# A decoder layer on one core: priority offsets by kind of result, rank-16 factors loaded early, other buffers for the last squares

## The chip, the cores and the metric

The kernel runs on one NeuronCore of a Trainium2 chip. The core has five engines that run side by side, each through its own instructions in order: TensorE (PE, matmuls; its weight loads, PEld, run beside them), VectorE (DVE), ScalarE (ACT), GpSimd (POOL) and SyncE (SP), which here only issues transfers. ScalarE can issue transfers too, on a queue of its own. The transfers of all queues run on 16 DMA engines. The metric is the device time of one execution in microseconds (us); lower is better.

## The reference

`x` and `ctx` are (8, 512, 256), float32. One layer of a decoder, with a layer norm behind each of three parts:

```python
x = _layernorm(x + _L0_attn_ref(x, W_q, W_k, W_v, W_g, W_o, log_decay))
x = _layernorm(x + _L0_xattn_ref(x, ctx, ctx, mask, Wq, bq, Wk, bk, Wv, bv, Wo, bo))
x = _layernorm(x + _L0_ffn_ref(x, fast_b, w_fc, w_proj, u, v, gate))
```

The first part is a gated linear attention within chunks of 32 positions, with a decay mask. The second is a softmax attention from x to ctx with 16 heads of 64. The third is the part that most of the change touches:

```python
scale = clip(mean(abs(w), axis=1), 1e-5)          # _bitlinear
tern = clip(round(w / scale), -1, 1)
y = x @ (tern * scale).T
h = _bitlinear(x, w_fc) + gate * (x @ v.T @ fast_b.T @ u.T)   # rank 16
r = maximum(h, 0)
out = _bitlinear(r * r, w_proj)
```

`u` is (1024, 16), `v` (16, 256), `fast_b` (16, 16), `gate` a scalar.

## The kernel before

Most float32 operands are split into two float16 halves, a high and a low one, and a product is three float16 matmuls (`PASSES`), accumulated in PSUM. So nearly every result of PE is followed by a cast (the high half, mostly ScalarE or GpSimd) and a subtraction (the low half, VectorE or GpSimd).

The work is cut by batch `b` (8), pair of heads `p` (8) and quarter of the queries `qt` (4): 256 units, which the code also calls steps. A unit has two score groups of 128 queries by 512 keys (`scores`: matmuls `s`, a VectorE reduction that adds the mask and finds the minimum `nm`, exponentials `e` on ScalarE), a split of the probabilities into halves `ph` (`split_p`), a DMA transpose of `ph` into `pT`, and the matmuls with the values, `av` (`attend`), which run about four units later. Around these units four "fillers" hand out other work in small pieces: the projections of keys, queries and values (`fr`), the first attention and the loads of the next batch (`bg`), the output projection and FFN of the batch before (`bf`), and a part of the last output projection (`bw`). `PULL` says how much of each is handed out per unit. In the first batch `bf` holds the set-up of weights instead: `setup_wo` and `setup_ffn`. `setup_ffn` makes the ternary weights (`fct`, `pjt`), a scale by an f32 matmul (`ps2`), and from the rank-16 factors `sv`, `gt`, `ur`, `fb` the two stationary operands `vst` and `ust`.

The code does not emit instructions in the order in which it is written. A `Recorder` collects every operation with a priority (`nc.prio`, counted in units: a lower value is earlier), then `schedule` plays the program through with a cost per operation (`cost`) and, whenever an engine is free, gives it the ready operation of lowest priority; an operation is ready when what it reads is there and its buffers are free. Where VectorE's next operation would have to wait for the memory port that it shares with GpSimd, another may go ahead of it whose priority is up to `REACH` later. The order found so is then emitted (that is why every row of the profile names line 451), and the hardware keeps it. So a constant in this planner has no cost of its own on the chip; it only changes the order. `LATE` holds offsets by kind of work (`c` scores, `a` attend, `t` the score reduction, `w` the set-up, `o` output projection, `f` FFN, `d` the transposes, and so on); the offsets `t`, `x` and `e` and everything added by the change hold only for operations with a priority of zero or more, and the set-up before the units has negative ones.

Buffers: a tile with a tag comes out of a ring of that tag with a fixed number of buffers, which SBUF rings hand out in program order. `tmp2` has four, `t4` five, `pT` and `ph` three each (a buffer of either holds 4,096 float16 values per partition), `E` three.

SP's queue carries all DMA transposes and nearly all loads, in the planner's order. ScalarE's queue carries six loads at the start. The end of the kernel is written out by hand behind the loop over the units: `bf.drain()`, the last `attend`s (`rest`), `wo_tail` (output projection, layer norm and transposes by PE) and `ffn_tail` for the two halves of the last batch's queries, interleaved by `go`; `TP` has the priorities of these parts. In `ffn_tail`, each of eight blocks `j` of the hidden dimension gives `r4` (relu, in an `E` buffer), its square, and the halves `rhl`, and three blocks later the matmuls `pyl` read them.

Of the kernel before, what the change touches and what calls it, by code (L numbers as in the profile page):

```python
# [11 lines left out]
F16 = mybir.dt.float16  # L12
F32 = mybir.dt.float32
# [8 lines left out]
HID, RANK = 1024, 16  # L22
# [4 lines left out]
LAG = 4  # L27
BURST = 2
MARGIN = 0.0
REACH = 9.52  # L30
SPARE = 1
DLATE = 1.6
PTS = 3
PHS = 3
NWP = 4
TP = (0.35, 0.96, 1.15, 3.0, 0.5, 5.1)
STICK = 2.09
HOLD = 0.18
HIGH = ("apaa", "paaa", "papp")
LATE = {"k": 0.0, "q": 0.0, "v": 0.53, "w": -0.33, "l": -0.41, "o": -0.91, "f": 0.31, "s": 0.0, "a": 0.91, "t": 0.0, "x": 0.31, "e": 0.0, "c": -1.28, "d": -0.95}  # L40
PULL = {"k": 5.13, "l": 2.62, "w": 3.61, "f": 4.71, "g": 5.48}

PASSES = ((0, 0), (0, 1), (1, 0))

# [109 lines left out]
class Recorder:  # L154
# [34 lines left out]
    def add(self, engine, method, args, kw):  # L189
        ins, outs = [], []  # L190
        for n, x in enumerate(args):
            if isinstance(x, View):
                (outs if n == 0 or (method == "tensor_tensor_reduce" and n == 7) else ins).append(x)
        for k, x in kw.items():
            if isinstance(x, View):
                (outs if k == "accum_out" else ins).append(x)
        o = Op()
        o.engine, o.method, o.args, o.kw, o.prio = engine, method, args, kw, self.prio
        if engine in ("DVE", "ACT") and method[:3] != "dma" and self.prio >= 0:
            src = ins[0].t if ins else None  # L200
            if method == "tensor_tensor_reduce":
                o.prio += LATE["t"]
            elif method == "activation" and args[2] == AF.Exp:
                o.prio += LATE["x"]
            elif src is not None and src.pool[:2] == "ps":
                o.prio += LATE["e"]
        o.preds, o.succs, o.bufs, o.parts = {}, [], [], None
        self.cost(o, ins, outs)
        if self.joint is not None and self.joint:
            j = self.joint[0]  # L210
            j.parts.append(o)
            self.access(j, ins, outs)
            return o
        o.seq = len(self.ops)
        self.ops.append(o)
        self.access(o, ins, outs)
        if self.joint is not None:
            o.parts = [o]
            self.joint.append(o)
        return o  # L220
# [30 lines left out]
    def cost(self, o, ins, outs):  # L251

        n = max([int(np.prod(x.shape[1:])) for x in outs + ins] or [0]) if o.engine != "PE" else outs[0].idx.size
        psum = any(x.t.pool[:2] == "ps" for x in ins + outs)
        ones = sum(x.idx.size == 1 and x.t.free > 0 for x in ins)
        o.half, o.port = None, o.engine == "POOL"
        o.dma = o.method[:3] == "dma"
        if o.dma:
            x = (outs or ins)[0]
            if o.method == "dma_start_transpose":  # L260
                blocks = n / 128
                o.occ, o.lat = 0.1 * blocks + 0.4, 0.115 * blocks + 0.55
            else:
                size = {F32: 4, F16: 2}.get(x.t.dt, 1)
                o.occ, o.lat = 0.45, n * size * x.shape[0] / (380e3 if self.prio < 0 else 210e3) + (1.2 if size == 1 else 0.1)
        elif o.engine == "PE":
            o.occ = n / 2400 + 0.0025
            o.lat = o.occ + 0.17
            if ins[0].p1 - ins[0].p0 == 64:
                o.half = ins[0].p0  # L270
        elif o.engine == "DVE":
            lat = 0.145 + n * 1.042e-3
            if o.method == "tensor_tensor_reduce":
                o.occ, o.lat = 0.615, 0.8
                return
            if not psum and o.method in ("tensor_copy", "tensor_scalar") and n >= 512:
                lat = 0.12 + n * 0.62e-3
            if psum and ones and o.method == "scalar_tensor_tensor":
                lat += 0.065
            if n <= 8:  # L280
                lat = 0.19 if o.method == "reciprocal" else 0.175 if o.method == "bn_aggr" else 0.145
            o.occ, o.lat = lat - 0.085, lat
            o.port = not psum and o.method in ("tensor_tensor", "scalar_tensor_tensor", "tensor_scalar", "tensor_copy")
        elif o.engine == "ACT":
            lat = 0.165 + n * 0.83e-3 + (0.0 if psum else 0.04) + 0.07 * ones
            o.occ, o.lat = (lat + 0.01, lat + 0.12) if "accum_out" in o.kw else (lat - 0.11, lat)
        elif o.engine == "POOL":
            if o.method == "tensor_tensor":
                lat = 0.3 + n * 1.67e-3 if n <= 512 else 0.2 + n * 1.9e-3
                if o.args[3] == ALU.pow:  # L290
                    lat = 0.42 + 0.16 * n
            else:
                lat = 0.13 + n * 0.9e-3 if n > 512 else 0.92 if n == 256 and o.kw == {} and o.method == "tensor_scalar" and o.args[-1] == ALU.is_lt else 0.62 if n > 256 else 0.56 if n > 8 else 0.22 + n * 5e-3
            o.occ, o.lat = lat - 0.03, lat
# [178 lines left out]
def decoder_kernel(ctx: ExitStack, tc: tile.TileContext, ins: dict, out: bass.AP):  # L473
    nc = Recorder(tc.nc, tc)
# [9 lines left out]
    def t4(name, shape, dt=F16):  # L484
        return wk.tile(shape, dt, tag="t4", name=name, bufs=5)

    def tmp2(name, shape, dt=F32):
        return wk.tile(shape, dt, tag="tmp2", name=name, bufs=4)
# [157 lines left out]
    def absmean(sc, th, src, n, width, nm):  # L646
# [4 lines left out]
        nc.vector.tensor_scalar(th[:, 0:n], sc, 0.5, None, ALU.mult)  # L651
        nc.vector.tensor_scalar(th[:, n:2 * n], sc, -0.5, None, ALU.mult)

    def setup_ffn():
        sfc = cst.tile([128, 8], F32, name="sfc")
        for i in range(2):
# [35 lines left out]
        pb = misc("ps2")  # L692
# [2 lines left out]
        yield 6  # L695

        nc.vector.memset(vst, 0.0)
        sv = tmp2("sv", [128, 2, RANK])
        nc.sync.dma_start(sv, ins["vT"].rearrange("(c p) r -> p c r", p=128))
        split(vst[:, :, 0:RANK], vst[:, :, 96:96 + RANK], sv, WS)  # L700
        for g in (32, 64):
            nc.vector.tensor_copy(vst[:, :, g:g + RANK], vst[:, :, 0:RANK])

        gt = cst.tile([128, 1], F32, name="gt")
        nc.sync.dma_start(gt, ins["gate"].broadcast_to([128, 1]))
        rs = cst.tile([128, 8], F32, name="rs")
        nc.vector.reciprocal(rs, sfc)
        nc.vector.tensor_scalar(rs, rs, gt, None, ALU.mult)
        ur = tmp2("ur", [128, 8, RANK])
        nc.sync.dma_start(ur, ins["u"].rearrange("(c p) r -> p c r", p=128))  # L710
        nc.vector.tensor_tensor(ur, ur, rs.unsqueeze(2).broadcast_to([128, 8, RANK]), ALU.mult)
        uh = tmp2("uh", [128, 2, 8, RANK], F16)
        split(uh[:, 0], uh[:, 1], ur, 1.0)
        fb = cst.tile([RANK, RANK], F32, name="fb")
        nc.sync.dma_start(fb, ins["fast_b"])
        fbs = cst.tile([RANK, 2, 128], F16, name="fbs")
        nc.vector.memset(fbs, 0.0)
        split(fbs[:, 0, 0:RANK], fbs[:, 1, 0:RANK], fb, 1.0)
# [311 lines left out]
    def ffn_tail(b, i, base, step_):  # L1030
        row = rows[b]
        rh, py = {}, {}
        ts = slice(256 * i, 256 * i + 256)
        PL = 3
        for s_ in range(8 + PL):
            nc.prio = base + step_ * s_
            if s_ == 0:
                zst = ffn_z(b, ts, f"{b}_{i}", ("zst", "sph")[i])
            if s_ < 8:
                j = s_  # L1040
                r4 = ffn_h(b, j, ts, zst, f"{b}_{i}", True)
                hl = t4(f"rhl{i}{j}", [128, 2, 256])
                if i == 0 or j % 2:
                    nc.scalar.activation(r4, r4, AF.Square)
                else:
                    nc.vector.tensor_tensor(r4, r4, r4, ALU.mult)
                if j % 2:
                    nc.scalar.copy(hl[:, 0], r4)
                else:
                    nc.vector.tensor_copy(hl[:, 0], r4)  # L1050
                (nc.vector if j % 3 == 2 or (i == 1 and j == 7) else nc.gpsimd).tensor_tensor(hl[:, 1], r4, hl[:, 0], ALU.subtract)
                rh[j] = hl
            if s_ >= PL:
                j = s_ - PL
                if j == 0:
                    for t in range(2):
                        py[t] = misc(f"pyl{i}{t}")[:, :D]
                hl = rh.pop(j)
                for t in range(2):
                    for a in range(2):  # L1060
                        nc.tensor.matmul(py[t], hl[:, a, t * 128:(t + 1) * 128], tpj[:, j, :],
                                         start=(j == 0 and a == 0), stop=(j == 7 and a == 1))
            yield
# [168 lines left out]
    for p in range(2):  # L1232
# [4 lines left out]
        if p == 0:  # L1237
            setup_qkv(2, 0, N1, 0)
            run_all(gen_v(0, 0))
    nc.prio = -1.0  # L1240
    for i in (1, 2, 0):
        setup_qkv(i, N1, HID, 0)
    nc.prio = 0.0
# [3 lines left out]
    def at(i, off):  # L1247
        now[0], nc.prio = i, i + off
# [84 lines left out]
            if pend:  # L1333
                attend(pend.pop(0))

    at(U, 1)
    bf.drain()
    at(U, TP[0])
    rest(len(pend) - 4)
# [63 lines left out]
```

## Time and profile before

| | us |
|---|---|
| median of 3 runs (1057.99 to 1062.4) | 1061.06 |
| the profiled execution: its own time | 1061.94 |
| its span, first to last instruction | 1060.1 |
| PE busy | 998.2 |
| VectorE busy | 986.9 |
| ScalarE busy | 879.4 |
| GpSimd busy | 544.8 |
| transposes pT, 131 of them: issue to landing, median | 7.5 |
| load of u: issued at 108.95, issue to landing | 3.9 |
| load of vT: issued at 108.3, issue to landing | 2.1 |

The loads of the gate and of `fast_b` are issued at 16.8 and 18.3 us. The profiled execution's granted TensorE clock is 0.988 of full speed on average.

How to read it: times in the trace start with the span. Busy time leaves out issuing, branching and waiting. A group of the profile is named engine, operation, output <- inputs, without buffer numbers. "Idle before" is the time that an engine stood still just ahead of an instruction, with what ended it; "issue" means that nothing which the profile shows was waited for. "PEld" waits are those of the weight loads, which run ahead of the matmuls. An average over the span hides that the stages differ: the set-up and first batch (to about 160 us), six batches of some 122 us each in steady running, and the end of the last batch (from about 1010 us).

### The profile page before, as it was taken

What the parts mean: (1) busy time and instruction counts of PE and PEld (TensorE: products, weight loads), DVE (VectorE), ACT (ScalarE), POOL (GpSimd) and SP (SyncE); (2) the same over time, 40 slices, a digit from 0 to 9 for tenths busy, and PEclk for the clock granted to TensorE, in tenths of its full rate; (3) what the DMA queues carried; (4) which work ended last, traced back from release to release, by engine and by line L of the source; (5) the groups of instructions that cost most, each with busy time, mean ns of one, the idle gap of its engine ahead of it and who ended that gap; (6) DMA issues with size and microseconds to landing.
All of it is one profiled execution on the core that took longest, in us unless ns stands there. A gap on an engine that the chain in (4) does not pass through costs nothing.

```text
span 1060.1 us, 29949 instructions
## 1 busy us (share of the span) xinstructions
PE 998.2 (94%) x11976; PEld 639.3 (60%) x11976; DVE 986.9 (93%) x2101; ACT 879.4 (83%) x1876; POOL 544.8 (51%) x513
## 2 busy tenths in 40 slices
PE   7986889999999999999999999999999999999986
PEld 4644545665666656665666656766567656665664
DVE  7999989999999989999899989999899998998976
ACT  7787778889977998789977898879977889878836
POOL 0251282256841596245861577426962548443635
PEclk9999989999999999999999999999999999999989
DMA  8289799999999999989999999999999999999861
GB/s 306 99 147 186 133 214 186 164 180 191 186 185 189 174 179 168 207 155 189 185 184 204 162 185 179 192 189 156 195 163 214 154 185 170 187 167 201 138 115 41
DMA packets 646636, 185.65 MB, mean 175 GB/s; under 512 B 628448, under 2 KB 641376, under 8 KB 646496
## 3 DMA queue, kind: packets, MB, share of 16 engines
q1 hardware_dynamic: 645632, 183.42, 95.6%
q8 instruction: 93, 1.52, 0.6%
q10 hardware_dynamic: 864, 0.32, 0.1%
q14 instruction: 47, 0.39, 0.1%
HBM read 21.18 MB, written 4.19 MB: 24 GB/s over the span
## 4 chain that ended last, share of the span: by engine, by line
PE 41%; ACT 17%; DVE 17%; DMA 12%; issue 6%; POOL 4%; SPq 2%; ACTq 0%; POOLq 0%; DVEq 0%
PE av L451 8%; PE s L451 8%; DMA pT<-ph 6%; ACT e L451 6%; DVE s L451 5%; DVE ph L451 5%; PE pk L451 4%; PE pq L451 4%; PE pwo L451 4%; ACT r L451 4%; PE py L451 3%; PE pvv L451 3%; ACT ph L451 3%; SPq L451 2%; DVE W L451 2%
## 5 line engine op out<-in xcount | busy, mean ns | idle before, releaser
L451 ACT ACTIVATE e<-s,nm 128x512 f32<-128x512 f32 x512 | 354.4, 705 | 100.7 <-DVE nm L451 83.3
L451 DVE SCALAR_TENSOR_TENSOR ph<-e,ph 128x1024 f16<-128x1024 f32 x256 | 330.6, 1298 | 27.6 <-ACT ph L451 25.2
L451 DVE CUSTOM_DVE_ANT_0 s<-s,mb 128x512 f32<-128x512 f32 x512 | 342.3, 710 | 6.1 <-PE s L451 4.5
L451 PEld LDWEIGHTS <-pT 128*128 128x128 f16 x6144 | 198.7, 99 | 59.5 <-issue 29.5
L451 PE MATMUL av<-v,pT 128*128 128x64 f16 x6144 | 213.2, 194 | 12.4 <-DMA pT<-ph 12.2
L451 PE MATMUL s<-W 64*128 64x512 f16 x1536 | 205.6, 379 | 12.5 <-ACT e L451 10.8
L451 ACT ACTIVATE ph<-e 128x1024 f16<-128x1024 f32 x186 | 200.0, 1081 | 2.4 <-DMA pT<-ph 0.3
L451 POOL TENSOR_SCALAR ph<-e 128x1024 f16<-128x1024 f32 x70 | 84.8, 1211 | 227.3 <-ACT e L451 214.7
L451 PEld LDWEIGHTS <-W 64*128 64x128 f16 x1536 | 64.2, 94 | 110.4 <-issue 59.4
L451 PEld LDWEIGHTS <-wqkv 128*128 128x128 f16 x768 | 70.3, 98 | 82.6 <-issue 18.0
L451 POOL TENSOR_TENSOR oh<-of,oh 128x512 f16<-128x512 f32 x62 | 86.6, 1396 | 65.0 <-ACT oh L451 63.1
L451 ACT ACTIVATION_READ_ACCUMULATOR e<-s,nm 128x1 f32 x512 | 113.5, 222 | 0.0
L451 PE MATMUL pk<-ctxh,wqkv 128*128 128x512 f16 x384 | 103.0, 382 | 6.2 <-POOL ctxh L451 6.1
L451 PE MATMUL pvv<-wqkv,ctxh 128*128 128x256 f16 x768 | 102.0, 274 | 0.3 <-DVE v L451 0.3
L451 POOL TENSOR_TENSOR rh<-r,rh 128x512 f16<-128x512 f32 x56 | 75.1, 1345 | 52.4 <-ACT rh L451 52.4
L451 PE MATMUL pq<-x1T,wqkv 128*128 128x512 f16 x384 | 97.2, 380 | 0.5 <-DVE bob L451 0.3
L451 PEld LDWEIGHTS <-ctxh 128*128 128x128 f16 x768 | 71.4, 98 | 26.1 <-issue 13.0
L451 PEld LDWEIGHTS <-oT 128*128 128x128 f16 x768 | 73.8, 100 | 20.8 <-issue 5.3
L451 PE MATMUL pwo<-wo,oT 128*128 128x256 f16 x672 | 84.2, 276 | 0.4 <-ACT e L451 0.4
L451 DVE DVE_READ_ACCUMULATOR2_ANT nm<- 128x1 f32 x512 | 72.4, 141 | 0.0
L451 PE MATMUL ph<-x2T,tfc 128*128 128x512 f16 (+1 forms) x288 | 68.4, 356 | 0.3 <-ACT r L451 0.3
L451 PE MATMUL py<-tpj,rh 128*128 128x256 f16 x448 | 58.4, 273 | 0.0
(190 smaller groups left out, 1492.4 us busy)
## 6 DMA issues: line engine op xcount, KB each, us to landing
row<-in_x SPq DMA_DIRECT2D x8, 512.0 KB, 5.4
xs<-in_xT SPq DMA_DIRECT2D x7, 512.0 KB, 4.9
ctxs<-in_ctxT SPq DMA_DIRECT2D x7, 512.0 KB, 4.5
out_dram<-row SPq DMA_DIRECT2D x7, 512.0 KB, 3.6
wqs<-in_wqkv SPq DMA_DIRECT2D x6, 512.0 KB, 7.2
pT<-ph SPq DMA_TRANSPOSE x131, 7.5
wos<-in_wo SPq DMA_DIRECT2D x4, 256.0 KB, 2.8
fcs<-in_w_fc SPq DMA_DIRECT2D x2, 512.0 KB, 4.9
```

The source lines that it names most:

```text
L451: getattr(real[x.engine], x.method)(*[r(a) for a in x.args], **{k: r(a) for k, a in x.kw.items()})
```

## The change

Four things. The planner adds an offset from a table `OFF` to every operation of priority zero or more, by engine and the letters of its first output's name (`"SP pT": 1.41` makes the transposes into pT count as 1.41 units later, `"DVE fct": -3.44` brings that kind forward). Other constants of the planner change with it: `REACH`, two entries of `LATE`, two of `PULL`, and `TP`, which gets a seventh entry for the priority ahead of `bf.drain()`. The planner's cost of a matmul with f32 operands becomes n/200 instead of n/2400 + 0.0025. The four loads of rank-16 factors leave SP's queue and the middle of `setup_ffn`; `load_rank` issues them on ScalarE's queue at priority -1, into tiles of their own instead of `tmp2` buffers (`gt` and `fb` had tiles of their own already). And in `ffn_tail` the sixteen `t4` tiles `rhl` become one tile per half of the queries, out of the `pT` ring for the first and the `ph` ring for the second.

```diff
-REACH = 9.52
+REACH = 11.86
...
-TP = (0.35, 0.96, 1.15, 3.0, 0.5, 5.1)
+TP = (-1.12, 2.0, 1.04, 3.04, 0.1, 5.1, 2.67)
...
+OFF = {"ACT th": -0.28, "ACT zst": -1.63, "ACT r": 0.81, "PE pTp": 1.99, "SP pT": 1.41, "ACT sph": 0.41, "DVE zf": 0.49, "PE ph": 0.16, "POOL ph": -1.37, "PE pwp": -0.46, "PE pTb": 2.45, "PE pb": 3.1, "POOL xh": 2.55, "ACT rh": 1.56, "PE pu": 0.39, "ACT row": 1.53, "PE po": -0.14, "PE pwl": 1.81, "SP xs": 0.62, "PE pss": -0.66, "DVE wqkv": -0.5, "DVE fct": -3.44, "ACT oh": -1.55, "DVE sp": 1.14, "POOL rhl": 0.12, "POOL oh": -0.82, "PE pyl": -0.58, "PE pz": -2.5, "PE pp": 0.13, "DVE mvb": -0.45}
-LATE = {"k": 0.0, "q": 0.0, "v": 0.53, "w": -0.33, "l": -0.41, "o": -0.91, "f": 0.31, "s": 0.0, "a": 0.91, "t": 0.0, "x": 0.31, "e": 0.0, "c": -1.28, "d": -0.95}
-PULL = {"k": 5.13, "l": 2.62, "w": 3.61, "f": 4.71, "g": 5.48}
+LATE = {"k": 0.0, "q": 0.0, "v": 0.53, "w": -0.48, "l": -0.41, "o": -0.91, "f": 0.31, "s": 0.0, "a": 0.91, "t": -0.55, "x": 0.31, "e": 0.0, "c": -1.28, "d": -0.95}
+PULL = {"k": 4.41, "l": 2.62, "w": 3.61, "f": 4.71, "g": 4.5}
...
+        if self.prio >= 0 and outs:
+            o.prio += OFF.get(engine + " " + re.split(r"[0-9_]", outs[0].t.name or "")[0], 0.0)
...
-            o.occ = n / 2400 + 0.0025
+            o.occ = n / 2400 + 0.0025 if ins[0].t.dt is F16 else n / 200
...
+    sv = cst.tile([128, 2, RANK], F32, name="sv")
+    ur = cst.tile([128, 8, RANK], F32, name="ur")
+    fb = cst.tile([RANK, RANK], F32, name="fb")
+    gt = cst.tile([128, 1], F32, name="gt")
+
+    def load_rank():
+        nc.scalar.dma_start(sv, ins["vT"].rearrange("(c p) r -> p c r", p=128))
+        nc.scalar.dma_start(ur, ins["u"].rearrange("(c p) r -> p c r", p=128))
+        nc.scalar.dma_start(fb, ins["fast_b"])
+        nc.scalar.dma_start(gt, ins["gate"].broadcast_to([128, 1]))
...
-        sv = tmp2("sv", [128, 2, RANK])
-        nc.sync.dma_start(sv, ins["vT"].rearrange("(c p) r -> p c r", p=128))
...
-        gt = cst.tile([128, 1], F32, name="gt")
-        nc.sync.dma_start(gt, ins["gate"].broadcast_to([128, 1]))
...
-        ur = tmp2("ur", [128, 8, RANK])
-        nc.sync.dma_start(ur, ins["u"].rearrange("(c p) r -> p c r", p=128))
...
-        fb = cst.tile([RANK, RANK], F32, name="fb")
-        nc.sync.dma_start(fb, ins["fast_b"])
...
+        rhl = wk.tile([128, 8, 2, 256], F16, tag=("pT", "ph")[i], name=f"rhl{i}", bufs=(PTS, PHS)[i])
...
-                hl = t4(f"rhl{i}{j}", [128, 2, 256])
+                hl = rhl[:, j]
...
     nc.prio = -1.0
+    load_rank()
...
-    at(U, 1)
+    at(U, TP[6])
     bf.drain()
```

## The prediction

> **What bounds the kernel now.** I read the page first: busy shares (part 1), then the slices (part 2), then the chain (part 4).
>
> ```profile
> PE 998.2 (94%) x11976; PEld 639.3 (60%) x11976; DVE 986.9 (93%) x2101; ACT 879.4 (83%) x1876; POOL 544.8 (51%) x513
> PE 41%; ACT 17%; DVE 17%; DMA 12%; issue 6%; POOL 4%; SPq 2%; ACTq 0%; POOLq 0%; DVEq 0%
> ```
>
> PE is idle for 1060.1 - 998.2 = 61.9 us and DVE for 73.2 us. No schedule can win more than PE's idle time, unless PE's own work gets denser. Where that time lies is in the table of busy time by stretch (columns: span, PE, PEld, DVE, ACT, POOL, clock, DMA share, GB/s):
>
> ```profile
> 0.00:26.50 26.50, 18.99 (x139) 12.12 (x140) 20.97 (x49) 20.12 (x42) 2.62 (x8) 1.00 0.88 306
> 26.50:53.00 26.50, 26.43 (x210) 16.86 (x208) 26.50 (x58) 20.10 (x44) 6.01 (x10) 1.00 0.29 100
> 53.00:80.00 27.00, 22.49 (x243) 11.90 (x243) 27.00 (x63) 22.70 (x60) 15.22 (x14) 1.00 0.84 148
> 80.00:106.00 26.00, 18.02 (x227) 11.09 (x225) 24.51 (x60) 20.19 (x43) 4.69 (x5) 0.94 1.00 185
> ...
> 500.00:600.00 100.00, 98.93 (x1246) 64.58 (x1245) 94.70 (x197) 85.21 (x180) 58.51 (x52) 1.00 1.01 183
> ...
> 1010.00:1020.00 10.00, 7.03 (x108) 5.76 (x107) 6.86 (x12) 2.40 (x7) 3.27 (x3) 0.83 1.21 192
> 1020.00:1030.00 10.00, 8.46 (x123) 6.12 (x122) 7.66 (x22) 4.32 (x10) 1.79 (x4) 0.90 0.24 44
> ```
>
> Three regimes are to be seen. From 26.5 to 107 us DVE is the bound (full, while PE is idle 4.5 and 8.0 us in two stretches). From 160 to 950 us PE is (idle 15.6 us in 790, adding up the ten stretches of the same answer). The end, from 1010 us, is a chain of short steps in which no engine is full.
>
> Last, the order of instructions at the two places where the rank-16 factors come in: ScalarE's start (its own queue's issues are "ACTq"), and VectorE around 103 to 113 us, where brackets give the idle time before a row and what ended it.
>
> ```profile
> 2.62 0.45 ACTq L451 DMA_DIRECT2D bk<-in_bk  x1
> 3.11 1.28 ACT L451 ACT_TABLE_LOAD   x1 [3.11 <-issue]
> 4.40 0.20 ACT L451 ACTIVATE ld<-ld 128x1 f32<-128x1 f32 x1
> ...
> 5.00 0.63 ACT L451 ACTIVATE wqkh<-wqk 128x512 f16<-128x512 f32 x1
> ```
> ```profile
> 6.61 0.58 PE L451 MATMUL pA<-wqkh,wqkh 128*128 128x256 f16 x2 [6.61 <-ACT wqkh L451]
> ...
> 102.96 1.20 PE L451 MATMUL ps<-dg,ones 128*128 128x256 f32 x2 [2.15 <-DVE dg L451]
> 103.95 2.65 PE L451 MATMUL av<-v,pT 128*128 128x64 f16 x48
> ```
> ```profile
> 104.19 0.42 DVE L451 COPY s2b<-ps 128x256 f32<-128x256 f32 x1 [0.71 <-PE ps L451]
> ...
> 109.78 0.70 DVE L451 CUSTOM_DVE_ANT_0 s<-s,mb 128x512 f32<-128x512 f32 x1 [0.89 <-PE s L451]
> ...
> 112.87 0.54 DVE L451 TENSOR_TENSOR ur<-ur,rs 128x128 f32<-128x128 f32 x1 [0.82 <-DMA ur<-in_u]
> ```
>
> **The change part by part.** The sum is made against the profiled execution: 1061.94 us, its span 1060.1 and 1.84 around it. It lies 0.88 above the median of the three runs (1061.06).
>
> *1. Rank loads at the start: +1.8.* The four loads wait for nothing, and ScalarE has nothing ready between its fifth issue (over at 3.07) and the first activation. The planner gives an engine whatever is ready, so I expect three of them ahead of the table load and the fourth just behind the tanh. An issue on this queue takes 0.42 to 0.46 us, so the four push the cast wqkh from 5.00 to about 6.8; I take 1.4 of the 1.84, since wqk itself lands only shortly before 5.00. PE's first matmul waits for that cast. Nothing later absorbs it: of PE's 7.5 us idle up to 26.5, 7.1 lie before 9.75, and from there to 53 us PE and VectorE are full. On the transfers: 95.6% of 16 engines' 1060.1 us over 645,632 packets is 25 ns a packet; some 1,280 rows of 64 bytes that used to come at 108 us are 2.0 us of all engines. The first stretch has 12% of 26.5 us = 3.2 us free, so I take 0.4. Ends: 0 (issues fit into gaps) and 1.84 + 2.0 = 3.8. On SP's queue the loads of gate and fast_b (0.66 and 0.34 us, in a stretch where SP waits anyway) and of vT and u (0.53 and 0.41) go; the next transpose is behind the latter, so up to 0.9 sooner, counted in step 2.
>
> A rule speaks against this step. The Trainium skill, "DMA: Bandwidth & Descriptors", section "Issuing engines are not separate DMA queues", says that all initiators share the same 16 DMA engines and that a second one saves only the time to initiate. By it, moving queues would be worth at most SP's 0.94 us for vT and u, against 1.84 on ScalarE: +0.9 by the rule alone. What the rule does not speak of is the earlier time of the load, which step 2 prices.
>
> *2. Loads and ring in the set-up, and the dearer f32 matmul: -1.7.* The stop at ur is 0.82 us of VectorE, and the chain spends 107.76 to 112.87 = 5.1 us on SP's two issues and the landing of u. sv and ur also leave the ring of four "tmp2" buffers that is handed out in order. The planner counted 0.11 us for each f32 matmul (256/2400 + 0.0025), and now 1.28; the trace shows two in 1.20 us, and VectorE standing 0.71 us for the result. That stop costs twice: the granted clock is 0.67 from 103 to 108 us, 48 av matmuls take 2.65 us there and 1.57 elsewhere, and VectorE then waits 0.89 for scores. Together 0.71 + 0.89 + 0.82 = 2.4 us of VectorE, the bound of this stage. I take 1.7: what is late next is the weight chain behind it (uT casts, ust), which ScalarE interleaves with exponentials. Ends: 0 and -5.1.
>
> A rule on that clock: "TensorE: Matmul & The Clock Gate", section "Part 1: The HAM clock gate (the "warmup" mystery)", puts the drop after an idle window of about 3.4 us. The rows have the clock down after waits of 1.65 and 2.15 us with matmuls between them, so shorter stops matter here. By the rule alone, the 1.1 us lost on the av matmuls would not be won back by shortening one wait, and the step would be -0.8 or so.
>
> *3. Squares of the last batch in the pT and ph rings: -0.5.* Sixteen pieces that went through five "t4" buffers become two tiles. No wait names a t4 buffer; the rows of rhl show ScalarE's r waiting 2.0 us in three pieces for the subtraction, which frees the square's own "E" buffer, and that ring stays at three. Ends: 0 and -2.0. A new wait could arise: rhl0 needs a pT buffer. The last av matmuls read pT at 1025.1, and the first square's cast starts at 1035.2, so 10 us cover it; the ph ring is free after the last transposes (about 1021).
>
> *4. The end: -2.5.* PULL["g"] from 5.48 to 4.5 pulls batch 6's 39 + 78 = 117 units of output projection and FFN over 26 of the last batch's units instead of 21, some 4.6 units of 3.8 us later. PE waits 2.28 us for a transpose (up to 1014.73) and is idle 2.97 + 1.54 = 4.5 us from 1010 to 1030 at a clock of 0.83 and 0.90; the matmuls py can fill some of that. Against it, two scalings (0.68 us) and four statistics (0.41), 3.0 us of VectorE, come into the tail, where VectorE is 67 to 78% busy from 1015 to 1053 us. TP moves the first half's projection 1.5 units ahead and the first half's FFN 1 behind; TP[6] does nothing, since the filler's drain sets the priority itself. Ends: -4.5 and +3.0.
>
> *5. Offsets in the steady part: -4.0.* PE's 15.6 us idle from 160 to 950 are the whole field. The named waits of PE there: 3.6 for POOL zh, 3.6 for POOL ctxh, 2.9 for ACT e, 2.6 for DMA pT, 1.4 for x2T. The offsets take POOL's ph and oh earlier and xh 2.55 units later, and LATE["t"] puts the score reductions half a unit ahead. I take a quarter of the field. A gain or a loss in PE's density is also open: six score matmuls take 0.75 us, twelve 1.40, so each pair brought together is worth 0.10 us. Ends: -15.6 and +16.5 (the transposes' offset, below).
>
> *6. The rest of the set-up, 53 to 160 us: -1.5.* PE is idle 21.7 us there, VectorE 7.8, of which step 2 used 2.4. The fct instructions come 3.4 units sooner and the bias matmuls pb (2.79 us of PE at 48.7) 3.1 later. VectorE's order changes, its work doesn't. Ends: -5.4 and +3.3 (what GpSimd's two bias additions take ahead of ctxh at 140.86, a wait that PE has already). The offset of DVE wqkv does nothing: those instructions have priorities below zero.
>
> Sum: +1.8 - 1.7 - 0.5 - 2.5 - 4.0 - 1.5 = -8.4, so 1061.94 - 8.4 = 1053.5, and 1052.7 from the median. I say 1053.
>
> **The rivals.** *Nothing in it, 1060.* The steady part has a period of 122 to 124 us a batch, which is PE's work; its last 1.5% could be irreducible, and the end could give back what it gets. Then 1061.9 + 1.8 - 1.7 - 0.5 - 1.5 = 1060. For it: PE at 98 to 99%; against it: the idle of the set-up and the end.
>
> *Slower, 1070: the transposes.* "SP pT" is 1.41 units (5.3 us) later in priority, so an oT transpose or a load can go ahead of a pT transpose. One oT issue is 1.26 us of SP. PE already waits 33 times for DMA pT, 33.5 us in both its queues, so these 33 have no slack. At 0.5 us more each: 16.5 - 8.4 = +8, so 1070. It decides from 8.4/33 = 0.25 us each, and is worse than the bound of measurement from 0.42 (13.7/33). For it: the DMA engines' share is 1.0 throughout; against it: the values' matmuls run about four units after issue.
>
> *Larger, 1044.* If the end's 4.5, half of the steady 15.6 and 5.4 of the set-up all go: 1061.9 + 1.8 - 4.5 - 7.8 - 5.4 - 1.7 = 1044.
>
> **How the numbers follow.** A measurement of this kernel can tell about 0.5% from no change, that is 1055.8 to 1066.4 around the median. Chances: the forecast 0.50 (its own range 1048 to 1058, of which 0.42 below 1055.8), larger 0.13, nothing 0.17, slower 0.20. Faster 0.42 + 0.13 = 0.55; within the bound 0.08 + 0.17 = 0.25; slower 0.20. The range, 1042 to 1068, leaves out the far part of the slower case and of the larger one.
>
> **What would show it.** Step 1: ScalarE's table load at 4.5 or later, PE's first matmul near 8. Step 2: no wait on ur, none of 2 us on dg, the clock above 0.9 from 100 to 115. Step 3: E-ring waits unchanged. Step 4: py matmuls after 1010, and more than 8.5 of 10 us busy there. Step 5: PE over 98.5% from 220 to 900. Wrong if the waits of PE on DMA pT pass 45 us, or PE's busy time itself rises.

## The result and the profile after

The changed kernel is slower by half a per cent: 1066.84 us median (1063.43 to 1069.31) against 1061.01 us (1057.16 to 1063.99) for the kernel before on the same chip. Over all executions the ratio is 1.0047, with a 95% interval from 1.0034 to 1.0059. The forecast was 1053, faster by 0.8%. The profiled execution took 1066.59 us, its span is 1064.8.

The page of the changed kernel, busy shares and chain:

```profile
PE 998.7 (94%) x11976; PEld 637.6 (60%) x11976; DVE 988.1 (93%) x2101; ACT 883.8 (83%) x1876; POOL 562.4 (53%) x513
PE 49%; DVE 22%; POOL 10%; DMA 7%; ACT 6%; issue 5%; SPq 0%; POOLq 0%; DVEq 0%; ACTq 0%
```

PE's busy time is the same to 0.5 us, so the work got neither more nor denser. The share of transfers in the chain fell from 12% to 7%; ScalarE's fell too, and those of PE, VectorE and GpSimd rose. The table of busy time by stretch, with the stretches shown of before (columns as there: span, PE, PEld, DVE, ACT, POOL, clock, DMA share, GB/s):

```profile
0.00:26.50 26.50, 16.06 (x120) 10.54 (x121) 16.89 (x42) 16.26 (x38) 1.07 (x6) 1.00 0.85 285
26.50:53.00 26.50, 24.68 (x187) 15.29 (x186) 26.22 (x57) 19.19 (x40) 7.68 (x12) 1.00 0.38 123
53.00:80.00 27.00, 23.41 (x217) 12.09 (x217) 27.00 (x60) 24.74 (x63) 13.75 (x12) 1.00 0.55 104
80.00:106.00 26.00, 18.64 (x241) 11.88 (x240) 23.09 (x61) 18.70 (x39) 8.36 (x7) 0.93 1.10 193
500.00:600.00 100.00, 98.27 (x1212) 63.98 (x1211) 94.37 (x200) 85.81 (x179) 58.31 (x53) 1.00 0.99 187
1010.00:1020.00 10.00, 9.96 (x143) 7.40 (x139) 10.00 (x21) 8.03 (x20) 8.77 (x7) 1.00 1.19 194
1020.00:1030.00 10.00, 10.00 (x186) 9.33 (x185) 8.47 (x17) 2.20 (x6) 4.14 (x5) 1.00 0.99 160
```

Two things are to be seen at once. The first stretch has 2.9 us less of PE and 4.1 us less of VectorE than before: everything starts later. And the gap of the end is closed: PE is busy 19.96 of 20 us at full clock, where it was busy 15.5 of 20 at 0.83 and 0.90.

**One account for all stretches.** A span is PE's work at full clock, plus PE's idle time, plus what PE loses at a lower clock. I take the idle time from the stretches, and count half of the PE-busy time that lies inside the trace's records of a granted clock of 0.5. What is left over, the work, is 988.5 us before and 987.8 after. So the two other terms say where the time went:

| stretch, us | idle before | idle after | half clock before | half clock after | difference |
|---|---|---|---|---|---|
| 0 to 40, the start | 7.5 | 10.7 | 0 | 0 | +3.2 |
| 40 to 240, set-up and behind it | 23.4 | 23.8 | 4.9 | 10.9 | +6.4 |
| 240 to 900, steady | 12.7 | 14.5 | 0 | 0 | +1.8 |
| 900 to the end | 18.4 | 17.1 | 4.8 | 0 | -6.1 |
| sum | 62.0 | 66.1 | 9.7 | 10.9 | +5.3 |

With the work's -0.7 that is the span's +4.7. The end gives what was hoped and more; the start and the set-up take one and a half times as much. Both columns are one execution each; how far the sizes hold over more of them is said with the experiments.

**The start.** ScalarE's first instructions after the change:

```profile
2.62 0.45 ACTq L454 DMA_DIRECT2D bk<-in_bk  x1
5.46 0.39 ACTq L454 DMA_DIRECT2D sv<-in_vT  x1
5.89 0.48 ACTq L454 DMA_DIRECT2D ur<-in_u  x1
6.93 0.34 ACTq L454 DMA_DIRECT2D fb<-in_fast_b  x1
7.31 1.28 ACT L454 ACT_TABLE_LOAD   x1 [7.31 <-DMA sv<-in_vT]
7.89 0.36 ACTq L454 DMA_DIRECT2D gt<-in_gate  x1
8.71 0.61 ACT L454 ACTIVATE wqkh<-wqk 128x512 f16<-128x512 f32 x1
...
10.22 0.59 PE L454 MATMUL pA<-wqkh,wqkh 128*128 128x256 f16 x2 [10.22 <-ACT wqkh L454]
```

Between bk's issue, over at 3.07, and sv's at 5.46 ScalarE does nothing, and in the kernel before bk is followed at once by the table load (3.11). The trace names the reason: each issue waits for a completion semaphore, a counter that tells of the landing of a load, and that an earlier load is still using. The times are from the records of issues and landings in the profiled execution of the changed kernel:

| issue | on the engine | waits for the landing of | which lands at, us | issued at, us |
|---|---|---|---|---|
| sv | ScalarE | wqk, first load | 5.44 | 5.46 |
| ur | ScalarE | ident | 5.69 | 5.89, right behind sv's issue |
| w0s, first load | SP | wqk, second load | 6.37 | 6.38 |
| fb | ScalarE | dif | 6.91 | 6.93 |
| gt | ScalarE | bk | 7.87 | 7.89 |

The table load stands behind fb's issue, over at 7.28; its bracket names sv's load only because that uses one of these semaphores. There are eight of them (100 and 102 to 108 in the trace). At the start the loads of SP's and ScalarE's queues together take them in turn, and a load that gets one already in use waits, on its engine, until the earlier load has landed. Before, ScalarE's five loads and SP's first three filled the eight, and only SP met a wait (its fourth load, until 4.21). The planner keeps eight loads in flight for each queue (`landed` in `schedule`), so this wait is not in its plan. SP's loads slip too: w0s from 5.00 to 6.38, the first row from 9.68 to 13.76.

**The set-up.** Two rows of the table by stretch, before:

```profile
80.00:120.00 40.00, 29.52 (x353) 17.30 (x351) 36.33 (x86) 29.82 (x64) 10.10 (x9) 0.96 0.98 176
120.00:160.00 40.00, 33.30 (x397) 20.47 (x396) 35.87 (x76) 28.70 (x60) 24.78 (x24) 0.91 0.93 180
```

and after:

```profile
80.00:120.00 40.00, 30.14 (x333) 17.45 (x334) 35.52 (x87) 29.59 (x62) 13.17 (x11) 0.84 1.08 196
120.00:160.00 40.00, 33.41 (x394) 21.00 (x389) 35.45 (x84) 28.79 (x61) 17.46 (x16) 0.86 0.77 149
```

PE is as busy as before, but at a clock of 0.84 and 0.86 in place of 0.96 and 0.91. The clock's records hold one stretch of 13.7 us at 0.5, from 113.9. The timeline of PE ahead of it and in it (start, duration, idle time before):

```profile
111.78 0.37 PE L454 MATMUL s<-W 64*128 64x512 f16 x1 [0.66 <-ACT uT L454]
112.63 0.80 PE L454 MATMUL s<-W 64*128 64x512 f16 x5 [0.47 <-ACT e L454]
...
114.15 0.58 PE L454 MATMUL pu<-identh,uh 128*16 128x128 f16 x4 [0.40 <-DVE of L454]
115.63 0.58 PE L454 MATMUL pz<-uT,fbs 16*128 16x512 f16 x1 [0.89 <-ACT e L454]
116.13 0.59 PE L454 MATMUL pu<-identh,uh 128*16 128x128 f16 x4
...
117.63 1.03 PE L454 MATMUL pz<-uT,fbs 16*128 16x512 f16 x2
118.59 2.74 PE L454 MATMUL s<-W 64*128 64x512 f16 x12
...
122.23 2.74 PE L454 MATMUL av<-v,pT 128*128 128x64 f16 x48
124.78 1.04 PE L454 MATMUL pk<-ctxh,wqkv 128*128 128x512 f16 x2
```

The prediction had 1.40 us for twelve score matmuls and 1.57 for 48 av; both take 2.74 here. VectorE, the bound of this stage, then stands for PE:

```profile
128.07 0.69 DVE L454 SCALAR_TENSOR_TENSOR row<-pp,row 128x512 f32<-128x512 f32 x1 [4.20 <-PE pp L454]
```

### The profile page after: what moved, and what is told of

The parts are those of the page before. It is cut to its first block, busy times and chain, and to the rows that moved or that the text cites. A ratio compares the mean times of both kernels' runs of the same rounds, so it can differ in the third digit from the quotient of the medians.

```text
span 1064.8 us, 29902 instructions
## 1 busy us (share of the span) xinstructions
PE 998.7 (94%) x11976; PEld 637.6 (60%) x11976; DVE 988.1 (93%) x2101; ACT 883.8 (83%) x1876; POOL 562.4 (53%) x513
## 4 chain that ended last, share of the span: by engine, by line
PE 49%; DVE 22%; POOL 10%; DMA 7%; ACT 6%; issue 5%; SPq 0%; POOLq 0%; DVEq 0%; ACTq 0%
PE s L454 9%; PE av L454 9%; DVE s L454 7%; PE pwo L454 6%; DVE ph L454 6%; DMA pT<-ph 5%; PE pk L454 5%; PE pvv L454 5%; PE pq L454 4%; PE py L454 3%; POOL row L454 2%; ACT e L454 2%; POOL xsa L454 2%; DVE W L454 2%; PE pxa L454 2%
## 5 line engine op out<-in xcount | busy, mean ns | idle before, releaser
L454 DVE SCALAR_TENSOR_TENSOR ph<-e,ph 128x1024 f16<-128x1024 f32 x256 | 334.3, 1309 | 23.0 <-ACT ph L454 21.2
L454 POOL TENSOR_SCALAR ph<-e 128x1024 f16<-128x1024 f32 x70 | 88.1, 1259 | 215.3 <-ACT e L454 195.4
L454 POOL TENSOR_TENSOR oh<-of,oh 128x512 f16<-128x512 f32 x62 | 99.1, 1599 | 98.5 <-ACT oh L454 97.8
L454 ACT ACTIVATION_READ_ACCUMULATOR e<-s,nm 128x1 f32 x512 | 109.6, 214 | 0.0
L454 PE MATMUL pk<-ctxh,wqkv 128*128 128x512 f16 x384 | 97.7, 382 | 12.5 <-POOL ctxh L454 9.7
L454 PE MATMUL pvv<-wqkv,ctxh 128*128 128x256 f16 x768 | 97.2, 273 | 0.2 <-ACT e L454 0.2
L454 PE MATMUL pwo<-wo,oT 128*128 128x256 f16 x672 | 81.8, 273 | 0.7 <-ACT e L454 0.5
L454 DVE DVE_READ_ACCUMULATOR2_ANT nm<- 128x1 f32 x512 | 69.9, 137 | 0.0
```

Source lines behind the costliest of these rows:

```text
L454: getattr(real[x.engine], x.method)(*[r(a) for a in x.args], **{k: r(a) for k, a in x.kw.items()})
```

## The experiments

Each kernel's ratio is to the kernel before, run on the same chip beside it. "Half clock" in the text is the term of the account above, from the one profiled execution. It varies from one execution to the next: the mean granted clock of the changed kernel's nine runs from 0.984 to 0.989, which is 5 us. Where a median over all executions is given, it is (1 - mean granted clock) x time, which counts stretches in which PE stood idle as well (14.9 us for the changed kernel, 11.7 for the one before).

**1. Does the start cost 3 to 4 us, and by the wait, not the bytes?** `a_late4` keeps the planned order of the changed kernel and, behind the planner, moves the four loads to just ahead of the first exponential (issued from 45.3 to 47.5 us), with the two ScalarE casts that read sv and fb a few instructions later:

```diff
         self.schedule()
+        late = [o for o in self.ops if o.dma and o.engine == "ACT" and o.args[0].t.name in ("sv", "ur", "fb", "gt")]
...
+        ops = ops[:k] + late + ops[k:]      # k: first exponential
+        self.ops = ops[:k] + moved + ops[k:]    # k: second exponential
```

> The changed kernel with its order kept, but the four rank-16 loads moved on ScalarE's queue to just ahead of the first exponential, and the two casts of them on ScalarE behind the next unit's. Theory A (ScalarE stands at its start for completion semaphores of earlier loads, and nothing absorbs it): PE's first matmul back from 10.2 to about 6.6 us, and 3.6 us less in all, about 1063. Rival B (the 3.6 us are absorbed later, and the loss is made in the set-up's clock alone): PE's first matmul near 6.6, but 1066 to 1067. Half-clock stretches between 90 and 155 us stay as they are in both (24 us in all).

`a_tiny4` does the same, but four loads of four bytes (the gate, into a tile that nothing reads) stand where the four were:

```diff
+    tn = cst.tile([1, 4], F32, name="tn")
+    nc.tiny = [(tn[:, i:i + 1], ins["gate"]) for i in range(4)]
```

> As the kernel with the four loads moved, but four loads of four bytes each, read by nobody, stand where the four loads were. Theory A1 (it is the wait for a free completion semaphore, whatever the size): PE's first matmul stays near 10.2 us and the time at about 1066. Rival A2 (it is the 64-byte rows in the DMA engines): PE's first matmul near 7 to 8 us, time 1063 to 1064.

`a_late4`: 1062.85 us, ratio 1.0017 (1.0001 to 1.0032). `a_tiny4`: 1066.32 us, ratio 1.0047 (1.0033 to 1.0062), as the changed kernel. The starts, `a_late4` first:

```profile
3.10 1.28 ACT L463 ACT_TABLE_LOAD   x1 [3.10 <-issue]
...
6.58 0.59 PE L463 MATMUL pA<-wqkh,wqkh 128*128 128x256 f16 x2 [6.58 <-ACT wqkh L463]
```
```profile
5.01 1.70 ACTq L472 DMA_DIRECT2D tn<-in_gate  x3
6.74 1.28 ACT L472 ACT_TABLE_LOAD   x1 [6.74 <-DMA dif<-in_diffmask]
...
9.65 0.58 PE L472 MATMUL pA<-wqkh,wqkh 128*128 128x256 f16 x2 [9.65 <-ACT wqkh L472]
```

Four loads of four bytes hold the first matmul until 9.65, against 6.58 without them and 10.22 with the real ones. So 3.1 of the 3.6 us come without the bytes, from the waits for shared completion semaphores with the issues among them, and at most 0.6 from the transfers (`b_rank`, below, has the real loads and its first matmul at 9.73, so it may be less). The whole is worth 3.2 us by the ratios (0.0030 of 1061) and 4.0 by the medians.

**2. The end by itself, and the loads by themselves.** `b_end` is the kernel before with the parts that touch the end alone, `b_rank` the kernel before with the four early loads alone:

```diff
 b_end
-TP = (0.35, 0.96, 1.15, 3.0, 0.5, 5.1)
+TP = (-1.12, 2.0, 1.04, 3.04, 0.1, 5.1, 2.67)
-PULL = {..., "g": 5.48}
+PULL = {..., "g": 4.5}
+        if self.prio >= 224 and outs:
+            o.prio += OFF.get(...)
+        rhl = wk.tile([128, 8, 2, 256], F16, tag=("pT", "ph")[i], ...)
 b_rank
+    def load_rank(): ...      # and the four loads in setup_ffn removed
     nc.prio = -1.0
+    load_rank()
```

> The kernel before with what the change does at the end alone: the tiles rhl in the pT and ph rings, TP, PULL g at 4.5, and the offsets for priorities of 224 and more. Theory C (the end is what the change gains: three half-clock stretches of 3.4 us between 963 and 1031 go, 5.1 us of clock): 1056. Rival D (the end's gain is only work that the changed set-up had put off): 1060 to 1062.

> The kernel before with the early loads on ScalarE's queue alone (and the tiles of their own), planned anew. Theory A: PE's first matmul at 10.2 instead of 6.6 us, and the kernel 2 to 4 us slower, 1063 to 1065, if the half-clock stretches of the set-up stay at three of 3.4 us. Rival (steps 1 and 2 of the prediction: +1.8 and -1.7): 1061.

`b_end`: 1057.64 us, ratio 0.9962 (0.9947 to 0.9976). It is faster than both kernels. `b_rank`: 1077.68 us, ratio 1.0149 (1.0123 to 1.0175), three times the whole change's loss and far above the 1063 to 1065 of theory A; its start costs about what it costs in the changed kernel (first matmul at 9.73), and the order that the planner then finds adds 12 us more.

`a_late4` and `b_end` have the same parts of the change at the end, and neither loses at the start. `a_late4` is slower by 5.2 us in the medians and 5.8 by the ratios, whose intervals lie apart. If the end gains the same in both, that is what the changed kernel loses in the set-up and the steady part together; the account of one execution had 8.2. The half clock over all executions is 14.9 us in the median in `a_late4` and 9.5 in `b_end`, so about as many microseconds more.

The gain of the end was split twice: `b_end_nooff` leaves out the offsets from unit 224 on, `b_end_norhl` leaves the squares in their `t4` buffers.

> The kernel before with rhl in the other rings, TP and PULL g, and no offsets at all. Theory G (the end's gain is FFN work pulled later into the end, which keeps PE and its clock up): no half-clock stretch between 960 and 1040 us, 1057 to 1058. Rival H (the offsets make it): stretches come back and 1060 to 1062.

> Before with the end's times, PULL g and offsets from unit 224 on, but the squares still in their eight own buffers. Step 3 put the squares' move at 0.5: 1058. If the move matters to the end (squares no longer wait for the buffers of the hidden layer): 1059 to 1061.

`b_end_nooff`: 1059.18 us, ratio 0.9981 (0.9968 to 0.9995). `b_end_norhl`: 1057.16 us, ratio 0.9956 (0.9941 to 0.9972). By the middle values the times (`TP`, `PULL["g"]`) give about half and the late offsets the other half (the intervals of `b_end` and `b_end_nooff` overlap), and the squares' new buffers nothing that can be told. The gap after 1010 us in `b_end`, then in `b_end_norhl`:

```profile
1010.00:1020.00 10.00, 9.57 (x160) 8.72 (x158) 6.70 (x15) 1.93 (x6) 3.37 (x4) 1.00 0.96 152
1020.00:1030.00 10.00, 8.98 (x120) 7.38 (x116) 7.85 (x23) 5.90 (x14) 1.66 (x4) 1.00 0.01 2
```
```profile
1010.00:1020.00 10.00, 10.00 (x175) 9.32 (x172) 8.22 (x18) 2.74 (x7) 3.54 (x5) 1.00 0.84 133
1020.00:1030.00 10.00, 8.98 (x101) 7.22 (x99) 7.91 (x25) 5.90 (x15) 2.39 (x6) 1.00 0.00 0
```

**3. Is it the offsets that spoil the set-up?** `a_off48` is the changed kernel with `OFF` only from unit 48 on.

```diff
-        if self.prio >= 0 and outs:
+        if self.prio >= 48 and outs:
```

> The changed kernel, but the offsets hold only for priorities of 48 and more, so not in the set-up and first batch and a half. Theory E (the offsets make the set-up's work on PE sparse, and the clock halves): half-clock time between 85 and 160 us falls from 24 to 10 us or less, PE's first matmul stays at 10.2, time 1060 to 1062. Rival F (it is the earlier rank chain, the f32 cost and the other constants): half-clock time there stays at 17 us or more, 1065 to 1068.

1067.92 us, ratio 1.0057 (1.0035 to 1.0078): no better. Without the offsets the set-up, planned anew once more, is about as bad (31.5 us of idle and half-clock time from 40 to 240, 34.7 in the changed kernel).

**4. Is the half clock the cause of the loss in the set-up?** Two kernels add 168 matmuls (identity by identity, 128 columns, read by nobody) over units 4 to 31, six a unit, for the planner to place: `b_end_warm` on `b_end`, `a_late4_warm` on `a_late4`.

```diff
+        if 4 <= i < 32:
+            nc.prio = i + 3.0
+            ps = misc(f"warm{i}")
+            for _ in range(6):
+                nc.tensor.matmul(ps[:, 0:128], identh, identh, start=True, stop=True)
```

> The kernel before with the end parts, and 168 extra matmuls (identity by identity, 128 columns, a PSUM tile that nobody reads) at a priority three units late, in units 4 to 31, so that the planner puts them where PE has nothing to do. Theory I (the half-clock stretches of the set-up cost their lost clock in time): of four stretches of 3.4 us between 60 and 160 us at most one is left and the time falls by 3 to 6 us from 1057.6. Rival J (VectorE is the bound there, and PE's clock costs nothing, or the extra work gets into the way): 1057 to 1066, whatever the clock.

> The changed kernel with the four loads moved behind the start, and the same 168 extra matmuls. Theory I: the long half-clock stretch of 10 to 14 us after 110 us goes, and 4 to 8 us from 1062.9, so 1055 to 1059. Rival J: 1062 to 1070.

`b_end_warm`: 1067.02 us, ratio 1.0043 (1.0029 to 1.0057). `a_late4_warm`: 1061.44 us, ratio 0.9998 (0.9978 to 1.0018). Neither time lies in a range that was set for it, and neither run separates the clock: the planner made new orders around the extra work, PE's work rose by 12 us in the one (999.4 against `b_end`'s 987.6) and 10 in the other, and in `a_late4_warm` the idle time from 40 to 240 fell from 24.2 to 15.3 us beside the half clock (9.5 to 6.4).

`a_fill` keeps the order of the changed kernel, and so asks better. Behind the planner it adds 38 matmuls, repeats of those that stand there, each into what the next one overwrites, around the gaps that PE has between 111 and 116 us:

```diff
         self.schedule()
+            # PE's second and third group of rank transposes: four more of each;
+            # first matmul of the scores and of the rank product between: two more
+                for _ in range(more.get(x, 0)):
+                    y.kw = dict(start=True, stop=True)
+                    ops.append(y)
+                ops.append(x)
```

> After, its order kept, with 38 extra matmuls among those that surround the rank transposes (the second and third group of four transposes are issued five times over, the first matmul of the scores and of the rank product between them three times); each writes what the next one overwrites. They stand in the gaps that PE has there between 111 and 116 us. Theory K (the sparse chain there costs by the half clock that follows, 13.7 us from 113.9): that stretch falls to at most 3.4 us, time 1061 to 1064. Rival L (the stretch is not made by those gaps, or PE's speed there does not carry to the end): 1066 to 1068, stretch as before.

1067.89 us, ratio 1.0062 (1.0041 to 1.0083). The stretch goes, the time doesn't. The rows of the changed kernel in 5 us steps, then those of `a_fill`, then its PE timeline:

```profile
115.00:120.00 5.00, 4.37 (x17) 1.16 (x18) 4.58 (x8) 3.85 (x9) 4.73 (x4) 0.50 1.13 211
120.00:125.00 5.00, 5.00 (x59) 2.97 (x54) 3.78 (x9) 2.67 (x8) 0.59 (x1) 0.50 0.66 47
```
```profile
115.00:120.00 5.00, 4.83 (x60) 2.16 (x58) 5.00 (x11) 4.31 (x11) 4.80 (x4) 1.00 1.14 182
120.00:125.00 5.00, 5.00 (x76) 3.83 (x73) 4.37 (x11) 5.00 (x13) 0.38 (x1) 1.00 0.74 110
```
```profile
117.09 1.47 PE L475 MATMUL s<-W 64*128 64x512 f16 x12
...
119.03 1.57 PE L475 MATMUL av<-v,pT 128*128 128x64 f16 x48
```

So the first half of the reading holds: with the gaps filled the stretch at half clock is gone. Unfilled, the same order has 13.7 us of it, 10.2 in `a_late4` and 6.8 in `a_tiny4`; the half clock over all executions is 10.7 us in the median, against 14.9 in the changed kernel and in `a_tiny4`. The 128th exponential of the program comes 5.8 us sooner than in the changed kernel's profile but only 2.1 sooner than in `a_tiny4`'s, which has the same order and nearly the same start, so more than half of the 5.8 can be variation. The second half isn't shown: PE's work is 993.0 us in place of 987.8, and those 5.2 us eat nearly all of the 6.2 us that the half clock gave back from 40 to 240. The profiled execution is the third slowest of ten (1070.78); it lost the rest in the steady part (17.8 us idle from 240 to 900) and in two short stretches at half clock behind 939 us. Whether the clock could be held up for less than it costs stays open.

**5. Which part makes the set-up's order worse?** Three kernels are the changed kernel with one part back as it was: the loads (`a_oldload`), the f32 price (`a_f16cost`), the planner's constants (`a_oldconst`).

```diff
 a_oldload
-    load_rank()               # the four loads back in setup_ffn, on SP's queue, into tmp2 buffers
 a_f16cost
-            o.occ = n / 2400 + 0.0025 if ins[0].t.dt is F16 else n / 200
+            o.occ = n / 2400 + 0.0025
 a_oldconst
-REACH = 11.86
+REACH = 9.52
-LATE "w": -0.48, "t": -0.55;  PULL "k": 4.41
+LATE "w": -0.33, "t": 0.0;  PULL "k": 5.13
```

> After with the four rank loads back at their old places on SP's queue, in the temporary rings; offsets, constants and the f32 price stay. Theory F1 (it is the early rank loads that cost: 3.6 us at the start and the rest by the earlier chain they let the planner make in the set-up): 1057 to 1060, since only the end's gain of about 4 is left against before's 1061. Rival F2/F3 (the chain is innocent, the f32 price or the constants spoil the set-up): only the start comes back, 1062 to 1064, with the half-clock stretches between 105 and 128 still there. First matmul near 6.6 by both.

> After with the planner's old price for an f32 matmul (n/2400 for every type); all else stays. Theory F2 (the new price of the two f32 sums makes the set-up's order worse): 1060 to 1063. Rival F1: within 2 us of after, 1065 to 1069. The start stays at 10.2 for the first matmul by both.

> After with REACH, LATE w and t and PULL k at their old values; loads, offsets, f32 price and the end stay. Theory F3 (the planner's constants spoil the set-up): 1060 to 1063. Rival F1: 1065 to 1069. The start stays at 10.2 for the first matmul by both.

1075.56 us, ratio 1.0148 (1.0109 to 1.0187); 1068.05 us, 1.0062 (1.0046 to 1.0078); 1086.74 us, 1.0235 (1.0210 to 1.0260). None of the three theories holds: with any part taken out, the kernel is no faster, and twice much slower. So the remaining parts were run alone: the constants (`b_const`) and the offsets before unit 224 (`b_off`) on the kernel before, the f32 price on `b_end` (`b_end_f32`).

```diff
 b_const
-REACH = 9.52
+REACH = 11.86               # and LATE "w", "t", PULL "k" as in the change
 b_off
+        if 0 <= self.prio < 224 and outs:
+            o.prio += OFF.get(...)
 b_end_f32
+            o.occ = n / 2400 + 0.0025 if ins[0].t.dt is F16 else n / 200
```

> Before with REACH, LATE w and t and PULL k of after; nothing else. Theory G (the parts fit each other: the constants were settled together with the early loads and offsets, so that each alone makes a worse order than before's): 1064 or more. Rival H (each part adds its own share, and the constants by themselves are harmless or good): 1058 to 1062.

> Before with the offsets for units before 224 alone. Theory G: 1064 or more. Rival H: the offsets' share in the steady part and the set-up, 1056 to 1060 if the 4 to 5.5 us forecast for them are there, 1060 to 1062 if they do nothing.

> Before with the end's parts (1057.6) and the f32 price alone. By the forecast the price saves up to 1.7 with the loads: 1056 to 1058. Theory G: another order in the set-up with no reason to be better, 1058 to 1066, its own idle and half-clock time between 40 and 160 us above before's 22 and 5.

1070.77 us, ratio 1.0086 (1.0063 to 1.0110); 1094.20 us, 1.0298 (1.0272 to 1.0324); 1061.54 us, 0.9997 (0.9985 to 1.0009). Theory G's times are met by all three; of the two signs for `b_end_f32` one is there (7.3 us at half clock from 40 to 160, above 5) and one isn't (20.8 us idle, not above 22). The offsets alone cost 33 us and make the slowest kernel of all. Its two rows of the set-up:

```profile
80.00:120.00 40.00, 30.54 (x334) 18.10 (x333) 33.17 (x78) 25.78 (x57) 10.99 (x10) 0.83 0.78 143
120.00:160.00 40.00, 29.84 (x290) 16.51 (x287) 36.43 (x76) 26.97 (x58) 18.65 (x19) 0.84 0.84 167
```

All orders side by side, from the profiled executions (idle / half clock, us):

| kernel | ratio | 0 to 40 | 40 to 240 | 240 to 900 | 900 to the end | work |
|---|---|---|---|---|---|---|
| before | 1 | 7.5 / 0 | 23.4 / 4.9 | 12.7 / 0 | 18.4 / 4.8 | 988.5 |
| after | 1.0047 | 10.7 / 0 | 23.8 / 10.9 | 14.5 / 0 | 17.1 / 0 | 987.8 |
| b_rank | 1.0149 | 10.2 / 0 | 27.1 / 9.6 | 17.5 / 1.6 | 18.4 / 2.9 | 988.2 |
| b_const | 1.0086 | 8.0 / 0 | 26.2 / 12.4 | 14.5 / 0 | 15.7 / 3.3 | 988.4 |
| b_off | 1.0298 | 7.8 / 0 | 25.3 / 14.5 | 21.3 / 3.3 | 23.3 / 3.1 | 993.5 |
| b_end | 0.9962 | 8.0 / 0 | 22.0 / 6.4 | 14.2 / 0 | 17.4 / 0.5 | 987.6 |
| b_end_nooff | 0.9981 | 7.9 / 0 | 24.6 / 6.3 | 13.3 / 0 | 19.7 / 0 | 988.6 |
| b_end_norhl | 0.9956 | 7.0 / 0 | 24.1 / 4.8 | 13.1 / 0 | 17.4 / 0 | 987.7 |
| b_end_f32 | 0.9997 | 7.5 / 0 | 23.7 / 7.3 | 12.5 / 0 | 17.4 / 1.7 | 990.7 |
| a_off48 | 1.0057 | 10.3 / 0 | 23.5 / 8.0 | 15.0 / 3.4 | 17.4 / 2.7 | 986.5 |
| a_oldload | 1.0148 | 7.2 / 0 | 29.0 / 11.2 | 16.0 / 0 | 16.5 / 0 | 991.8 |
| a_f16cost | 1.0062 | 10.3 / 0 | 25.2 / 8.9 | 15.2 / 1.7 | 16.8 / 0 | 987.8 |
| a_oldconst | 1.0235 | 9.9 / 0 | 26.7 / 7.1 | 18.8 / 6.7 | 18.5 / 0 | 994.2 |

Alone, the four parts that reach the set-up cost 16.0 us (loads), 9.2 (constants), 32.6 (offsets) and 3.9 (f32 price, against `b_end`), medians against medians, 62 in all. The whole change costs 5.8 with the end's gain of some 4 in it, so about 10 without that gain. So the parts have no shares of their own that add up. No run changes the planner in a way that means nothing; whether any new order would be as much worse, with the one of before a fortunate one, is open. In the four kernels that leave the set-up of before nearly as it was (before and the three of the end), 40 to 240 us costs 28.3 to 30.9 us of idle and half-clock time; in the nine orders that plan it anew, 31.0 to 40.2. The least of these is `b_end_f32`, within the variation of one execution. The changed kernel's order has 34.7 in its own profile, 33.7 in `a_late4` and 31.8 in `a_tiny4`, so it loses some 3 to 6 us there, and the +6.4 of the account is at the upper end. Its half clock there is 9.4 to 10.9 us in the three, against 4.8 to 6.4 in the four that keep the set-up.

## Why the prediction was wrong

**Step 1, rank loads at the start, +1.8.** The place was right (three issues ahead of the table load, the fourth behind, nothing later that absorbs it), the term was mis-sized: +3.2 us of idle time in the account, first matmul +3.6. The step said "The four loads wait for nothing". They wait for completion semaphores that earlier loads still use; with the issues among them that is 3.1 us by `a_tiny4`. The upper end, 3.8, held.

**Step 2, loads and ring in the set-up, -1.7, and step 6, the rest of the set-up, -1.5.** These failed, and decided the sign: +6.4 by the account of one execution, some 3 to 6 over three executions of the same order, in place of -3.2. The two stops named are gone, as step 2 said (no wait on ur, none on dg). But the step took the rest of the stage's order as it stood. The planner made a new one: the rank transposes and their products now stand at 108 to 122 us (114 to 123 before) among short pieces of PE work, and the half clock from 40 to 240 rose from 4.9 to 10.9 us. The bound set at the outset, that no schedule can win more than PE's idle time, left the clock out: of PE's 998.2 us busy, 9.7 were already lost at half clock. The sign set as a test, a clock above 0.9 from 100 to 115, came out at 1.00, 0.70 and 0.84 in its three steps of 5 us, and at 0.50 from 115 to 125. PE's idle time in the stage is the same as before (23.8 and 23.4 us), so the loss isn't in how long PE stands. That filling the gaps ahead of the long stretch lifts its clock is shown by `a_fill`, that this saves time is not; why every new order of the set-up came out worse than the one of before is not.

**Step 3, squares in other buffers, -0.5.** Nothing: `b_end` and `b_end_norhl` are at 0.9962 and 0.9956, their intervals lie over each other.

**Step 4, the end, -2.5.** Right, and too small: -6.1 in the account with step 3, and -4.0 by `b_end` (0.0038 of 1061). The lower end was -4.5. What the step had counted only as idle time also brought the clock: the 4.8 us at half clock behind 960 us are gone.

**Step 5, offsets in the steady part, -4.0.** Wrong: PE's idle time from 160 to 950 is 19.1 us (the same ten stretches added up) in place of 15.6, and from 240 to 900 the account has +1.8. The loss is within what the same order varies (12.7 us in the kernel before, 13.1 to 14.2 in the three of the end); what is shown is that the gain isn't there. A quarter of that field was a share without a mechanism.

**The rivals.** The slower one named the wrong mechanism: the transposes' waits fell (PE's two queues wait 27.8 us for pT, before 33.5), its bound was never near. "Nothing in it, 1060" had the steady part right and kept the set-up's gain. What was missing was the case that happened: the new order of the set-up is worse than the old one, and more of it lies at half clock. The range's upper end, 1068, held the time by luck: it was set for the case of the transposes.

## What to carry to other kernels

A planner's constants have no separate prices. Here parts that cost 62 us one by one cost about 10 together, and taking one out gained nothing; so price a changed plan by the stage that it plans anew, and try the parts that reach only one stage (here the end, -0.4%) by themselves. Before a load is moved to an idle queue, count all loads in flight over all queues against the completion semaphores that they share: the issue itself can block the engine. And an account of idle time and half-clock time by stretch, whose remainder is the same in both kernels, shows in one table where a re-planned order lost.

## What the runs showed that was not expected

The half clock comes in stretches of 3.4 us and multiples of it (the last one is cut by the kernel's end), and can stay on while PE is full. In the changed kernel it holds from 113.9 to 127.6, though PE has not one gap from 116.13 on; in `a_late4` a stretch of 10.2 us from 111.0 runs on to 121.2 with no gap from 111.54 on. The Trainium skill, "TensorE: Matmul & The Clock Gate", section "Part 1: The HAM clock gate (the "warmup" mystery)", puts the return to the full clock after one busy window of about 3.4 us. The length of the steps agrees with that; that three such windows with PE busy went by at 0.5 does not. The matmuls in them use 16 or 64 rows or 64 columns in part; whether that counts as little activity was not tried, but in `a_fill` the same ones run at full clock from 115 to 125 (the rows above).

For one and the same order, the time varies with the clock. Over the changed kernel's executions the mean granted clock runs from 0.989 at 1063.4 us to 0.984 at 1069.3 us: (0.989 - 0.984) x 1066 = 5.3 us of clock for 5.9 us of time.
